# Layer statistics from ScalarE sums, with token routing moved three scan steps, in a two-layer fp32 kernel

## The chip, the cores and the metric

One Trainium2 chip, one of its cores. The metric is the device time of one execution in microseconds (us); lower is better. PE is TensorE, DVE is VectorE, ACT is ScalarE, POOL is GpSimd, and SP is the engine that only issues DMAs.

## The reference, cut to what matters

Eight sequences of 512 tokens with 256 features go through two layers in fp32. Each layer is attention and then a mixture of eight experts, both behind an adaptive layer norm:

```python
h = _layernorm(x) * (1 + ca) + sa
x = x + ga * _L0_attn_ref(h, ...)      # delta rule: a scan over the 512 tokens
h = _layernorm(x) * (1 + cb) + sb
x = x + gb * _L0_ffn_ref(h, ...)       # top-1 expert of 8, 256 -> 1024 -> 256
h = _layernorm(x) * (1 + ca) + sa
x = x + ga * _L1_attn_ref(h, ...)      # causal softmax attention with relative bias
h = _layernorm(x) * (1 + cb) + sb
x = x + gb * _L1_ffn_ref(h, ...)       # all 8 experts, weighted
```

The scan of layer 0 cannot be split over tokens: every step reads the state that the step before it wrote,

```python
retrieved = jnp.einsum('bnhd,bnd->bnh', M, k_t)
delta = v_t - retrieved
M = M + b_t[..., None, None] * jnp.einsum('bnh,bnd->bnhd', k_t, delta)
```

and `_layernorm` subtracts the mean of a token's 256 features and divides by sqrt(variance + 1e-5).

## The kernel before, in words

**Layer 0** goes by chunks of 128 tokens of all eight sequences, i = 0 to 3. `scan` (L731) makes one chunk's 128 steps on DVE. A step is four dependent instructions: a product (L741), a sum over it (L745), an outer product (L751) and the state's update (L756). Everything else of layer 0 is cut into pieces and hung on the steps: `run` (L1366) takes a list of (place, piece), and after step s it traces the pieces whose place is at most s. Within such a piece only the DVE instructions are tied to the step (`tc.issue_after(step)`); they may not come ahead of it. The other engines take theirs from a queue in an order that a list scheduler fixes when the kernel is built: mostly the order of the trace, with a later piece ahead where its inputs and its PSUM bank are free earlier by the scheduler's own estimate. [...] Seven PSUM banks serve all pieces in turn (`bank`).

While chunk i is scanned, three things share its steps:

- `front(i + 1)` normalizes and projects the next chunk's tokens, two sequences at a time: `stats(p)` at place 47 + 8p (sums on ACT, L498 to L509, ending in the square root `sda`), `normal(p)` six places later on DVE (L525), `turn` and `project` behind it. So normal(p) lies at places 53, 61, 69 and 77.
- `follow(i - 1)` does the chunk before: `attend` (places 0 to about 50; `rest` adds the branch to `x1` on POOL at 25 to 28 and 42 to 45, `stats` takes each row block's mean and variance on DVE at 30 to 33 and 46 to 49), then `route`, which is a generator with six parts at places 34, 42, 51, 57, 60 and 62: norm, transposes and gate logits of sequences 0 to 3 and of 4 to 7, the argmax and a prefix count. The last part yields the slots, and `scatter` sends the rows to DRAM by expert. Then `experts` works 15 tiles of 128 rows: `fetch` (L1149, POOL) gathers a tile's two weight blocks of about 1 MB each, `turn` loads and transposes the rows, L1195 and L1204 make the hidden layer, L1216 the output; L1221 copies it to SBUF on ACT, L1222 adds the bias on POOL, L1223 stores it to `ys`. Of the 15 tiles 11 (12 for chunk 2) start in the same scan at place 70 + 4.6 j (4.3 j), the others in the next one.
- The last chunk's `follow(3)` has no scan to hide in and runs in a stretch of its own (the tail of layer 0), together with what is left of chunk 2's experts and with the gathers (L1235) that bring each chunk's `ys` back into token order, multiply by the gate (L1271) and add to `x2` in DRAM (L1272). The gathers of chunks 0 and 1 use eight rows of one tile; those of chunk 2 use `yrow`, a tile with two buffers, with one row in flight (`DEPTH`).

**Layer 1** goes by sequences b: 16 steps of `scores`, `turn` and `weigh`, with `prologue(b + 1)` and `tail(b - 1)` hung between them. `tail` normalizes heads and projects them (`project`, POOL adds L1549, L1550), takes statistics of all four row blocks at place 6.6 (`statistics`, L120 to L134), makes the features (L172 to L183) and gate logits (L1568) from 7.6 on, then the weights at 14 and `experts(i)` (L1621, L1626) from 17 on. Sequence 7's tail comes after the last step; the experts of sequence 6 (places 135, 136.9, 138.8 and 148.8 in its count) lie between its pieces, which start at 134.

Of the kernel before, what the change touches and what calls it, by code (L numbers as in the profile page):

```python
# [20 lines left out]
B = 8  # L21
# [42 lines left out]
def tile_two_layers(ctx: ExitStack, tc: tile.TileContext, t: dict, out: bass.AP):  # L64
# [213 lines left out]
    with ExitStack() as l0:  # L278
# [477 lines left out]
                yield nc.vector.tensor_sub(M, M, upd).ins  # L756


        DEPTH = (3, 3, 1, 1)


        issued = {}
# [1 line left out]
        def attend(i, qk, V, x1, norms):  # L764
# [180 lines left out]
            def stats(b):  # L945
                h = b // 4
                if b % 4 == 0:
                    got["mv", h] = fp.tile([P, 4, 2], F32, tag="mvf", name=f"mvf{i}_{h}")
                st = fp.tile([P, 6], F32, tag="stf", name=f"stf{i}_{b}", bufs=4)
                nc.vector.bn_stats(st, x1[b])  # L950
                nc.vector.bn_aggr(got["mv", h][:, b % 4, :], st)
                if b % 4 == 3:
                    norms.append((got["mv", h], deviation(fp, "f", got["mv", h])))

            pieces = [(0, deltas), (1, tokens)]
            for b in range(B):
# [9 lines left out]
            for h in range(2):  # L966
                pieces.append((16 * h + 25, lambda h=h: roots(h)))
                for b in range(4 * h, 4 * h + 4):
                    pieces.append((13 * h + 25 + b, lambda b=b: rest(b)))
                    pieces.append((12 * h + 30 + b, lambda b=b: stats(b)))  # L970
            return got, pieces

        def route(i, h, norms):
# [29 lines left out]
                room = room.rearrange("p s a b -> p (s a b)")  # L1003
                turned_back = [room[:, b * D : (b + 1) * D] for b in range(B)]
            for half in range(2):
                rs, off = scale_offset(fp, "f", *norms[half])
                pl = bank()
                turned = None
                for n in range(5):
                    b = 4 * half + n  # L1010
                    if n < 4:
                        hb = xn[b]
                        nc.scalar.activation(
                            hb, h[b], AF.Identity, bias=off[:, n : n + 1], scale=rs[:, n : n + 1]
                        )
                        pt = bank()
                        for c in range(2):
                            nc.tensor.transpose(
                                pt[:, c * P : (c + 1) * P], hb[:, c * P : (c + 1) * P], ident
                            )  # L1020
                        hT = fp.tile([P, 2, P], F32, tag="hTf", name=f"hTf{i}_{b}", bufs=2)
                        for c in range(2):
                            by, plus = scale[0][:, 1, c, b : b + 1], shift[0][:, 1, c, b : b + 1]
                            if i == NT - 1 and c == 1:
                                nc.vector.tensor_scalar(
                                    hT[:, c, :], pt[:, c * P : (c + 1) * P], by, plus,
                                    ALU.mult, ALU.add,
                                )
                            else:
                                nc.scalar.activation(  # L1030
                                    hT[:, c, :], pt[:, c * P : (c + 1) * P], AF.Identity,
                                    bias=plus, scale=by,
                                )
                    if n > 0:
                        for k in range(2):
                            nc.tensor.matmul(
                                pl[:, (n - 1) * NE : n * NE], turned[:, k, :], gw[:, k, :],
                                start=(k == 0), stop=(k == 1),
                            )
                        back = bank()  # L1040
# [15 lines left out]
                if half == 0:  # L1056
                    yield
# [81 lines left out]
        def experts(i, slot, idx, scatter):  # L1139
# [46 lines left out]
            for j in range(NSLOT):  # L1186
# [31 lines left out]
                        start=(f == 0), stop=(f == NFC - 1),  # L1218
                    )
                ysb = fp.tile([P, D], F32, tag="ysb", name=f"ysb{i}_{j}", bufs=2)  # L1220
                nc.scalar.copy(ysb, py[:, :D])  # L1221
                nc.gpsimd.tensor_add(ysb, ysb, w[:, NFC * D :])  # L1222
                nc.gpsimd.dma_start(ys_d[i][j * P : (j + 1) * P, :], ysb)  # L1223
                if j != NSLOT - 3:
                    fetch(j + 2, 0)
                if i == NT - 1 and j == NSLOT // 2:
# [32 lines left out]
            queue = []  # L1259
            for b in range(B + DEPTH[i]):  # L1260
                if b < B:
                    if i < NT - 2:
                        yr = w1["fetched"][:, b * D : (b + 1) * D]
                    else:
                        yr = fp.tile([P, D], F32, tag="yrow", name=f"yrow{i}_{b}", bufs=2)
                    with tc.issue_after(issued["fetch"]):
                        gather(b, yr)
                    queue.append(yr)
                if b >= DEPTH[i]:
                    yr, k = queue.pop(0), b - DEPTH[i]  # L1270
                    nc.gpsimd.tensor_mul(yr, yr, gates[1][:, k, :])  # L1271
                    nc.gpsimd.dma_start(x2d[k][i], yr, accum_op=ALU.add)  # L1272
                yield

        def follow(i, qk, V):


            x1, norms = [], []
            _, pieces = attend(i, qk, V, x1, norms)
            work = {}  # L1280

            def begin():
                work["route"] = route(i, x1, norms)
# [12 lines left out]
            def behind():  # L1296
                with tc.issue_after(issued["attention"]):
                    on()

            pieces += [(34, begin), (42, more), (51, more), (57, more), (60, more), (62, settle)]  # L1300

            late, pace, starts = {
                NT - 1: (0, 4, [(10 * j, 10 * j + 3) for j in range(NSLOT)]),
                NT - 2: (12, 4.3, [(43, 62.1), (62.2, 62.4), (62.5, 62.7)]),
            }.get(i, (11, 4.6, [(8, 11), (22, 25), (40, 43), (62.2, 62.7)]))
            pieces += [(62.3, on), (62.6, on)]
            rest = []
# [115 lines left out]
    with ExitStack() as l1:  # L1425
# [76 lines left out]
        def tail(b, got):  # L1502
# [48 lines left out]

                nc.sync.dma_start(y2d[b][i], xs[:, i, :])

            def statistics():
                if b == B - 1:
# [4 lines left out]
                else:  # L1560
                    hT.append(lp.tile([P, 2, S], F32, tag="hTd", name=f"hTd{b}", bufs=1))
                stats.update(enumerate(row_stats("d", [xs[:, i, :] for i in range(NT)])))

            def logits(i):
                cols = slice(i * P, (i + 1) * P)
# [72 lines left out]
            yield from ((7.6 + k, piece) for k, piece in enumerate(made))  # L1638
            yield 14, weights
            yield 15.4, weights_T  # L1640

# [150 lines left out]
```

## Time and profile before

| | |
|---|---|
| median of 3 runs | 2165.22 us (2160.56 to 2169.86) |
| the profiled execution's own time | 2157.99 us |
| its span | 2156.3 us |
| mean granted PE clock | 0.883 |
| PE busy | 1698.6 us (79%) |
| DVE busy | 1577.8 us (73%) |
| ACT busy | 1078.8 us (50%) |
| POOL busy | 641.0 us (30%) |

The profiled execution lies 7.2 us under the median of the runs. Times in the profile count from the start of the span. The scans of chunks 0 to 3 start at 52.0, 298.2, 554.5 and 813.3 us and the last ends at 1067 us; the tail of layer 0 goes on to about 1310 us, and layer 1 fills the rest. In a listing, "out<-in" are tiles by name, brackets hold the engine's idle time before an instruction and what ended it, and a busy digit is tenths of one of 40 slices (53.9 us each).

### The profile page before, as it was taken

To read this page: it belongs to the slowest core of one execution; us is meant where nothing else is said; L and a number is where in the kernel's file an instruction comes from. 1 tells how busy PE (TensorE), PEld (TensorE's weight loads), DVE (VectorE), ACT (ScalarE), POOL (GpSimd) and SP (SyncE) were. 2 spreads that over 40 slices of the span, in tenths; PEclk is the share of its full clock that TensorE was granted. 3 is DMA by queue.
4 is the path that set the end of the run, shared out by engine and by line. 5 is a ranking of instruction groups with operands and counts; after the bars stand their busy time and mean duration, and the time that the engine had idled before them with its cause. 6 is when DMAs were issued, how large, how long until landed. Compare 5 with 4: busy or idle time off the path is not lost. (4 is left out here: it accounts for less than half of the span.)

```text
span 2156.3 us, 32495 instructions
## 1 busy us (share of the span) xinstructions
PE 1698.6 (79%) x10882; PEld 1193.8 (55%) x10882; DVE 1577.8 (73%) x4523; ACT 1078.8 (50%) x2674; POOL 641.0 (30%) x922
## 2 busy tenths in 40 slices
PE   5332137479786997849898798999999999999988
PEld 4211125369674786639777685555555555555543
DVE  4999999989989899899762004677676766776754
ACT  4253125474356744513343236776656574747431
POOL 1223014265354653623365643010111101010220
PEclk8666567699897998959998999999999999999998
DMA  5110000178202681118775873000101010000111
GB/s 169 50 51 5 0 1 11 33 258 303 77 14 81 252 325 50 48 69 321 238 128 196 274 241 74 1 20 9 29 13 25 14 23 13 23 16 11 19 20 14
DMA packets 88679, 189.62 MB, mean 88 GB/s; under 512 B 13712, under 2 KB 67152, under 8 KB 75712
## 3 DMA queue, kind: packets, MB, share of 16 engines
q0 software_dynamic: 33696, 137.43, 19.9%
q1 hardware_dynamic: 54816, 50.11, 8.1%
q8 instruction: 86, 1.41, 0.3%
q14 instruction: 81, 0.66, 0.1%
HBM read 175.12 MB, written 36.93 MB: 98 GB/s over the span
## 5 line engine op out<-in xcount | busy, mean ns | idle before, releaser
L1459 ACT ACTIVATE pr<-sc,low 128x384 f32<-128x384 f32 (+3 forms) x512 | 255.4, 555 | 183.2 <-DVE low L1454 180.8
L1454 DVE CUSTOM_DVE_ANT_0 sc<-ps,strips 128x384 f32<-128x384 f32 (+3 forms) x512 | 225.2, 485 | 95.1 <-PE ps L1445 63.4
L1195 PE MATMUL ps<-hTs,w 128*128 128x128 f32 x1920 | 242.5, 288 | 16.3 <-DMA w<-in_wrows,idx 11.2
L1195 PEld LDWEIGHTS ps<-hTs,w 128*128 128x128 f32 x1920 | 237.6, 203 | 24.2 <-issue 12.2
L745 DVE TENSOR_REDUCE state<-terms 128x16 f32<-128x272 f32 x512 | 227.3, 444 | 15.5
L1216 PE MATMUL ps<-w,act 128*128 128x256 f32 x960 | 226.5, 391 | 15.1 <-DMA w<-in_wrows,idx 12.4
L756 DVE TENSOR_TENSOR state<-state,upd 128x256 f32<-128x256 f32 x511 | 222.4, 435 | 15.0
L1621 PE MATMUL ps<-ew,hTd 128*128 128x512 f32 x512 | 230.5, 605 | 0.0
L741 DVE TENSOR_TENSOR terms<-state,K 128x256 f32<-128x256 f32 x512 | 216.2, 422 | 14.7
L751 DVE TENSOR_TENSOR upd<-K,state 128x256 f32<-128x256 f32 x511 | 214.4, 420 | 16.0
L1216 PEld LDWEIGHTS ps<-w,act 128*128 128x128 f32 x960 | 184.1, 197 | 41.5 <-issue 7.9
L1204 ACT ACTIVATE act<-ps,w 128x128 f32<-128x128 f32 x480 | 136.6, 371 | 139.4 <-PE ps L1195 138.4
L1471 PE MATMUL ps<-cst,pr 128*128 128x128 f32 x1280 | 189.2, 292 | 17.6 <-DVE low L1454 14.5
L1471 PEld LDWEIGHTS ps<-cst,pr 128*128 128x128 f32 x1280 | 146.8, 147 | 86.2 <-DVE low L1454 27.2
L1626 DVE SCALAR_TENSOR_TENSOR accd<-ps,wtd,accd 128x256 f32<-128x256 f32 x256 | 123.5, 482 | 78.0 <-PE ps L1621 70.6
L1630 POOL TENSOR_TENSOR accd<-accd,bc_g 128x256 f32<-128x256 f32 x28 | 20.4, 728 | 527.6 <-DVE accd L1626 527.6
L1621 PEld LDWEIGHTS ps<-ew,hTd 128*128 128x128 f32 x512 | 97.2, 194 | 113.6 <-issue 101.6
L1149 POOL DMA_INDIRECT w<-in_wrows,idx x120 | 123.8, 1032 | 100.0 <-ACT hTs L1173 38.8
L1445 PE MATMUL ps<-kT,qTc 32*128 32x128 f32 (+3 forms) x1024 | 130.6, 486 | 3.8 <-DVE low L1454 2.1
L1480 DVE COPY prT<-ps 128x512 f32<-128x512 f32 (+3 forms) x256 | 117.1, 484 | 8.7 <-PE ps L1471 8.2
L1478 ACT COPY prT<-ps 128x512 f32<-128x512 f32 (+3 forms) x256 | 98.6, 413 | 6.6 <-PE ps L1471 5.8
L1492 PE MATMUL ps<-prT,v 128*32 128x512 f32 (+3 forms) x1024 | 97.5, 452 | 0.0
(297 smaller groups left out, 2855.1 us busy)
## 6 DMA issues: line engine op xcount, KB each, us to landing
hs<-zero SPq DMA_DIRECT2D x4, 1920.0 KB
hslot<-hs SPq DMA_DIRECT2D x60, 128.0 KB
ys<-ysb POOLq DMA_DIRECT2D x60, 128.0 KB, 4.6
x<-in_x SPq DMA_DIRECT2D x32, 128.0 KB
strips<-strip_d SPq DMA_DIRECT2D x16, 256.0 KB
out<-accd POOLq DMA_DIRECT2D x32, 128.0 KB, 3.0
wm<-in_wmod SPq DMA_DIRECT2D x4, 768.0 KB
xt<-in_x SPq DMA_DIRECT2D x12, 256.0 KB
```

The source lines that it names most:

```text
L741: nc.vector.tensor_mul(term[:, :, :HD], M, K[:, s, :].unsqueeze(1).to_broadcast([P, HD, HD]))
L745: nc.vector.tensor_reduce(delta, term, AX.X, ALU.add)
L751: nc.vector.tensor_mul(upd, K[:, s, :].unsqueeze(2).to_broadcast([P, HD, HD]), delta.unsqueeze(1).to_broadcast([P, HD, HD]),)
L756: yield nc.vector.tensor_sub(M, M, upd).ins
L1195: nc.tensor.matmul(ph[:, q * P : (q + 1) * P], w[:, k * FF + f * P : k * FF + (f + 1) * P], hT[:, k, :], start=(k == 0), stop=(k == 1),)
L1204: nc.scalar.activation(act[:, f, :], ph[:, q * P : (q + 1) * P], AF.Relu, bias=w[:, 2 * FF + f : 2 * FF + f + 1],)
L1216: nc.tensor.matmul(py[:, :D], act[:, f, :], w[:, f * D : (f + 1) * D], start=(f == 0), stop=(f == NFC - 1),)
L1445: made = nc.tensor.matmul(pscs[r][:, :W], qT[rows, g, o, i * P : (i + 1) * P], kT[rows, g, :W], start=True, stop=True,)
L1454: nc.vector.tensor_tensor_reduce(out=sc[:, :W], in0=pscs[r][:, :W], in1=strips[:, n, S - W :], scale=1.0, scalar=3.0e38, op0=ALU.add, op1= ...
L1459: nc.scalar.activation(pr, sc[:, :W], AF.Exp, bias=low, scale=-1.0)
L1471: nc.tensor.transpose(pt[:, (i - j) * P : (i - j + 1) * P], prs[r, i][:, j * P : (j + 1) * P], ident,)
L1621: nc.tensor.matmul(pe, hT[0][:, k, cols], ew[:, k, e : e + 2, :], start=(k == 0), stop=(k == 1),)
```

## The change

1. In chunks 0 to 2, `stats` leaves DVE. For each pair of row blocks ACT makes a Copy pass with a running sum, scales the sum to minus the mean, makes a Square pass with that as bias and a running sum, and after four blocks one square root. These pieces lie at 34, 36, 50 and 52.
2. In chunks 0 to 2 the parts of `route` lie at 37, 46, 54, 61, 63 and 65, and what follows moves with them: the first fetches at 65.3 and 65.6, the tiles at 71.5 + 4.6 j (4.3 j), the leftover tiles' pieces that lay between 62.1 and 62.7 at 65.1 to 65.7.
3. The gathers of chunk 2 use eight rows of one tile (`rows`), with two rows in flight.
4. The last tile of chunk 3 adds its bias on DVE straight from PSUM, and SP stores it.
5. In the tail of sequence 7 the statistics come in two halves, at 3.6 and 5.6, and the features start at 4.2.

```diff
-        DEPTH = (3, 3, 1, 1)
+        DEPTH = (3, 3, 2, 1)
...
-                st = fp.tile([P, 6], F32, tag="stf", name=f"stf{i}_{b}", bufs=4)
-                nc.vector.bn_stats(st, x1[b])
-                nc.vector.bn_aggr(got["mv", h][:, b % 4, :], st)
-                if b % 4 == 3:
-                    norms.append((got["mv", h], deviation(fp, "f", got["mv", h])))
+                mv = got["mv", h]
+                if i == NT - 1:
...
+                elif b % 2:
+                    less = bank()
+                    pair = slice(b % 4 - 1, b % 4 + 1)
+                    for k in (b - 1, b):
+                        nc.scalar.activation(
+                            less[:, (k % 2) * D : (k % 2 + 1) * D], x1[k], AF.Copy,
+                            accum_out=mv[:, k % 4, 0:1],
+                        )
+                    nc.scalar.mul(mv[:, pair, 0], mv[:, pair, 0], -1.0 / D)
+                    for k in (b - 1, b):
+                        nc.scalar.activation(
+                            less[:, (k % 2) * D : (k % 2 + 1) * D], x1[k], AF.Square,
+                            bias=mv[:, k % 4, 0:1], accum_out=mv[:, k % 4, 1:2],
+                        )
+                    if b % 4 == 3:
+                        sd = fp.tile([P, 4], F32, tag="sdf", name=f"sdf{i}_{h}")
+                        nc.scalar.activation(
+                            sd, mv[:, :, 1], AF.Sqrt, bias=ln_eps, scale=1.0 / D
+                        )
+                        norms.append((mv, sd))
...
-                    pieces.append((12 * h + 30 + b, lambda b=b: stats(b)))
+                    wait = 3 if i < NT - 1 else 0
+                    pieces.append((12 * h + 30 + b + wait, lambda b=b: stats(b)))
...
-                rs, off = scale_offset(fp, "f", *norms[half])
+                if i == NT - 1:
+                    rs, off = scale_offset(fp, "f", *norms[half])
+                else:
...
+                    nc.vector.reciprocal(rs, sd)
+                    nc.vector.tensor_mul(off, mv[:, :, 0], rs)
...
-                nc.scalar.copy(ysb, py[:, :D])
-                nc.gpsimd.tensor_add(ysb, ysb, w[:, NFC * D :])
-                nc.gpsimd.dma_start(ys_d[i][j * P : (j + 1) * P, :], ysb)
+                rows = ys_d[i][j * P : (j + 1) * P, :]
+                if (i, j) == (NT - 1, NSLOT - 1):
+                    nc.vector.tensor_add(ysb, py[:, :D], w[:, NFC * D :])
+                    nc.sync.dma_start(rows, ysb)
+                else:
...
-                    if i < NT - 2:
-                        yr = w1["fetched"][:, b * D : (b + 1) * D]
-                    else:
-                        yr = fp.tile([P, D], F32, tag="yrow", name=f"yrow{i}_{b}", bufs=2)
+                    room = w1["fetched" if i < NT - 2 else "rows"]
+                    yr = room[:, b * D : (b + 1) * D]
...
-            pieces += [(34, begin), (42, more), (51, more), (57, more), (60, more), (62, settle)]
+            if i == NT - 1:
+                routing = (34, 42, 51, 57, 60)
+            else:
+                routing = (37, 46, 54, 61, 63)
+            pieces += zip(routing, (begin, more, more, more, more))
+            pieces.append((62 if i == NT - 1 else 65, settle))
...
-                NT - 2: (12, 4.3, [(43, 62.1), (62.2, 62.4), (62.5, 62.7)]),
-            }.get(i, (11, 4.6, [(8, 11), (22, 25), (40, 43), (62.2, 62.7)]))
-            pieces += [(62.3, on), (62.6, on)]
+                NT - 2: (12, 4.3, [(43, 65.1), (65.2, 65.4), (65.5, 65.7)]),
+            }.get(i, (11, 4.6, [(8, 11), (22, 25), (40, 43), (65.2, 65.7)]))
+            pieces += [(65.3, on), (65.6, on)]
...
-                        pieces.append((70 + pace * (j + half / 2), on))
+                        pieces.append((71.5 + pace * (j + half / 2), on))
...
-            yield 6.6, statistics
+            if b == B - 1:
+                yield 3.6, lambda: statistics((0, 1))
+                yield 5.6, lambda: statistics((2, 3))
+                begin = 4.2
+            else:
+                yield 6.6, lambda: statistics(tuple(range(NT)))
+                begin = 7.6
```

More of the change, by code (lines that the diff above doesn't have):

```diff
@@ L948, in stats @@
                     got["mv", h] = fp.tile([P, 4, 2], F32, tag="mvf", name=f"mvf{i}_{h}")
[L949 to L953 removed]
+                mv = got["mv", h]
+                if i == NT - 1:
+                    st = fp.tile([P, 6], F32, tag="stf", name=f"stf{i}_{b}", bufs=4)
+                    nc.vector.bn_stats(st, x1[b])
+                    nc.vector.bn_aggr(mv[:, b % 4, :], st)
+                    if b % 4 == 3:
+                        norms.append((mv, deviation(fp, "f", mv)))
+                elif b % 2:
[12 more added lines that the diff above has]
+                        )
+                    if b % 4 == 3:
+                        sd = fp.tile([P, 4], F32, tag="sdf", name=f"sdf{i}_{h}")
[3 more added lines that the diff above has]
+                        norms.append((mv, sd))
             pieces = [(0, deltas), (1, tokens)]
@@ L1005, in route @@
             for half in range(2):
-                rs, off = scale_offset(fp, "f", *norms[half])
+                if i == NT - 1:
+                    rs, off = scale_offset(fp, "f", *norms[half])
+                else:
+                    mv, sd = norms[half]
+                    rs, off = (
+                        fp.tile([P, 4], F32, tag=f"{tag}f", name=f"{tag}f{i}_{half}")
+                        for tag in ("rs", "off")
+                    )
+                    nc.vector.reciprocal(rs, sd)
+                    nc.vector.tensor_mul(off, mv[:, :, 0], rs)
                 pl = bank()
@@ L1220, in experts @@
                 ysb = fp.tile([P, D], F32, tag="ysb", name=f"ysb{i}_{j}", bufs=2)
-                nc.scalar.copy(ysb, py[:, :D])
-                nc.gpsimd.tensor_add(ysb, ysb, w[:, NFC * D :])
-                nc.gpsimd.dma_start(ys_d[i][j * P : (j + 1) * P, :], ysb)
+                rows = ys_d[i][j * P : (j + 1) * P, :]
[3 more added lines that the diff above has]
+                else:
+                    nc.scalar.copy(ysb, py[:, :D])
+                    nc.gpsimd.tensor_add(ysb, ysb, w[:, NFC * D :])
+                    nc.gpsimd.dma_start(rows, ysb)
                 if j != NSLOT - 3:
@@ L1552, in project, with statistics @@
                 nc.sync.dma_start(y2d[b][i], xs[:, i, :])
-            def statistics():
-                if b == B - 1:
+            def statistics(tiles):
+                if not hT and b == B - 1:
                     hT.append(
@@ L1559, in statistics @@
                     )
-                else:
+                elif not hT:
                     hT.append(lp.tile([P, 2, S], F32, tag="hTd", name=f"hTd{b}", bufs=1))
-                stats.update(enumerate(row_stats("d", [xs[:, i, :] for i in range(NT)])))
+                tag = "d" if len(tiles) == NT else "c"
+                stats.update(zip(tiles, row_stats(tag, [xs[:, i, :] for i in tiles])))
             def logits(i):
@@ L1637, in tail @@
             )
-            yield from ((7.6 + k, piece) for k, piece in enumerate(made))
+            yield from ((begin + k, piece) for k, piece in enumerate(made))
             yield 14, weights
```

## The prediction

> **What bounds the kernel now.** I read the page first. The scan lasts from 52 to 1067 us, and there DVE is near full in every slice:
>
> ```profile
> DVE  4999999989989899899762004677676766776754
> ACT  4253125474356744513343236776656574747431
> ```
>
> The second row says that ACT, which is to take over work, is about half busy there. Being near full is not yet a price, so next the DVE timeline of a scan step with a statistics pair and, after "...", of the end of a bare one (columns: start, length, engine, line, operation):
>
> ```profile
> 916.52 0.43 DVE L756 TENSOR_TENSOR state<-state,upd 128x256 f32<-128x256 f32 x1
> 916.86 0.41 DVE L950 BATCH_NORM_STATS2 stf<-x 128x6 f32<-128x256 f32 x1
> 917.20 0.41 DVE L741 TENSOR_TENSOR terms<-state,K 128x256 f32<-128x256 f32 x1
> 917.52 0.17 DVE L951 BATCH_NORM_AGGREGATE mvf<-stf 128x2 f32<-128x6 f32 x1
> ...
> 918.57 0.43 DVE L756 TENSOR_TENSOR state<-state,upd 128x256 f32<-128x256 f32 x1
> ...
> 920.62 0.43 DVE L756 TENSOR_TENSOR state<-state,upd 128x256 f32<-128x256 f32 x1
> 921.09 0.42 DVE L741 TENSOR_TENSOR terms<-state,K 128x256 f32<-128x256 f32 x1
> ```
>
> L756 to L756 is 2.05 us with a pair (916.52, 918.57, 920.62); bare steps are 1.86 us apart. So a pair whose instructions last 0.41 and 0.17 us lengthens a step by 0.19 us. L756 to L741 is 0.47 us bare and 0.68 us with L950 between: the chain waits for its own results, and an independent instruction mostly fills that wait.
>
> Third, the waits of DVE during the scans of chunks 1 to 3 (total, times, longest):
>
> ```profile
> DVE rsa L525 <- ACT sda L509: 9.7, 5, 4.9
> DVE dm L930 <- POOL bdM L931: 4.8, 4, 1.4
> DVE ms L934 <- ACT ms L919: 4.0, 3, 2.0
> ```
>
> The longest are two waits of normal(3) for `sda`: 4.86 us at 461.2 (chunk 1) and 3.65 us at 720.5 (chunk 2). ACT's timeline ahead of the first:
>
> ```profile
> 450.09 1.14 ACT L1204 ACTIVATE act<-ps,w 128x128 f32<-128x128 f32 x4 [3.87 <-PE ps L1195]
> 452.36 1.14 ACT L1204 ACTIVATE act<-ps,w 128x128 f32<-128x128 f32 x4 [1.13 <-PE ps L1195]
> ...
> 453.58 0.40 ACT L498 ACTIVATE ps<-xt 128x256 f32<-128x256 f32 x1
> ...
> 460.87 0.29 ACT L509 ACTIVATE sda<-mva,cst 128x2 f32<-128x2 f32 x1
> ```
>
> stats(3), at place 71, stands behind the first tile's activations, at place 70, which wait for PE.
>
> From 1067 us on PE takes over: it is busy 58.4 of 64 us (1066 to 1130), then 119.2 of 136 us (1170 to 1306). In that last stretch POOL and PE wait for:
>
> ```profile
> POOL yrow L1235 <- DMA x<-yrow: 10.9, 4, 5.4
> POOL yrow L1271 <- DMA yrow<-ys,slot: 4.5, 3, 3.2
> ```
> ```profile
> PE ps L1195 <- DMA w<-in_wrows,idx: 7.7, 6, 4.5
> PE ps L1216 <- DMA w<-in_wrows,idx: 7.2, 3, 3.5
> ```
>
> POOL issues the weight fetches, so its stalls make them late. Layer 1 is PE's (713.9 of 737 us); the change touches only its end, where PE idles 6.03 us for sequence 7's statistics:
>
> ```profile
> 2103.51 0.69 PE L179 MATMUL ps<-cst,xnd 128*128 128x128 f32 x2 [6.03 <-ACT xnd L172]
> ```
>
> **What the Trainium skill says.** "VectorE: DVE Perf Modes", section The DRAIN you can't avoid, says that the next operation does not start until the pipe is empty, and to minimize the count of operations. By that, 24 pairs at 0.59 us would give 14 us; the intervals above give a third, and I take the trace. "ScalarE: Activation LUTs", section Table sets, says that cheap functions are in every set, so Copy and Square need no load; the trace agrees (L498 and L504 have none of their own; a load of L509 lasts 1.283 us). "DMA: Bandwidth & Descriptors", section Anatomy of one DMA, gives about 2.0 us fixed; the last `ys` store takes 1307.07 to 1309.09, 2.02 us.
>
> **The change part by part.**
>
> *Statistics off DVE.* 8 pairs in each of three chunks, at 0.19 us: 1.5 us a chunk. Reciprocal and product stay (0.17 and 0.15 us). In chunks 1 and 2 (the scans in which chunks 0 and 1 are routed) it is on the path: -3.1. In chunk 3 PE sets the end: nothing there.
>
> *The same on ACT.* A row block costs what L498 and L504 with their accumulator reads show, spaced 0.31 + 0.22 + 0.41 + 0.22 = 1.16 us: 4.8 us a half with the small ones. It lands where ACT was idle: 7.8 us at 356 to 364, 13.6 us waiting for the last L951 (387 to 401), 6.1 us in the next scan. Behind it in the queue are attention's copies; cover gone, a half would cost up to 4.8 us. I take 0.
>
> *Routing three steps later, chunks 1 and 2.* The first tile moves from 70 to 71.5, behind stats(3) at 71, and its data come 3 x 1.86 = 5.6 us later. stats(3) needs only its bank and `xt`, so ACT should take it first: of 4.86 + 3.65 = 8.5 us I take -7.0 (0 to -8.5). In exchange, half 1 of the gate (8 us of ACT work, 404.7 to 413.8) slides from 51 to 54, onto stats(1), whose `sda` was already 0.3 to 0.4 us late at place 61. And argmax to prefix count shrinks from three steps to two, leaving PE some 1.2 us for a matmul pair that now takes 0.8 us behind other work. No row shows either; up to 5.6 us a scan for the first, below nothing since attention's last pieces now precede the gate (the `ms` waits of these two scans, 2.0 and 1.0 us, could go). The scheduler put rows late where it expected inputs late, so I take +2.0 (-3 to +11).
>
> POOL's eight scatters and first fetches (10 us) and SP's row loads move along; tiles then run to about place 121 of 128, so only the start of the next scan gets PE work, where PE idles.
>
> *Routing later, chunk 3.* PE is full from the first tile (969.4) to the scan's end and into the tail, so a late start is paid in full. The slots were ready at 946.9, but POOL stood before tile 14's output (L1222 at 950.05) and began to scatter at 951.92. Slots 5.6 - 1.5 = 4.1 us later come at 951.0: nothing lost, unless tile 14 slips too; then up to 5.6. I take +2.0.
>
> *Rows and depth.* POOL's 15.4 us of gather stalls go. The PE waits directly behind them are 3.5 (fetch issued 1203.0 after a stall of 5.4) and 4.5 us (fetch issued 1229.4 after one of 4.0); others follow transfers that took 7 to 8 us without a stall. If DMA bandwidth is the limit, nothing is won: 0 to -9, I take -4.5.
>
> *Last bias.* After the last L1216 (1305.5) come ACT's copy, POOL's add (1306.05, 0.72 us) and POOL's issue at 1307.07. One DVE add (0.42 us, as L1548, also from PSUM) and SP's issue (0.32) would start the store at about 1306.15: -0.9. DVE and SP have nothing else then (DVE is busy 3.3 of the last 136 us), and the gather behind it is on the path: PE idles 4.88 us until 1315.55 for its rows. If the SP store landed later than POOL's, this could be 0.
>
> *Halves.* Block 1's `xs` is done at 2091.4, so blocks 0 and 1 get their norm while sequence 6's experts hold PE (2089.6 to 2096.5). After the last `xs` at 2101.4 only blocks 2 and 3 are left. PE's first transpose stays at 2103.5; the copies of four blocks, 1.67 us apart, now end at 2110.1, 6.6 us later; those of two, back to back from 2104.2 at 0.8 us each, would end at 2105.9: -4.2 (-2 to -5). Behind that come the gate logits, then experts, all shifted as one. Next late is block 3 itself. One more root and reciprocal (0.3 and 0.2 us) lie in ACT's and DVE's idle time.
>
> Sum: -3.1 - 7.0 + 2.0 + 2.0 - 4.5 - 0.9 - 4.2 = **-15.7 us**, so 2158.0 becomes 2142.3; on the median, 7.2 us higher, 2165.2 becomes **2149.5**.
>
> **Rivals.**
>
> *The moves cancel* (stats(3) freed, stats(1) late by as much). For: ACT is busy almost without a break from 413 to 428. Against: DVE's order is the scheduler's. Without the terms -7.0 and +2.0 of the scans: -10.7, 2154.5.
>
> *Nothing reaches the end but halves and bias*: DMA-bound fetches, tile 14 slipping, waits as they were: -3.1 + 5.6 - 0.9 - 4.2 = -2.6, 2162.6. That the change does not do what it says has this look too: the scheduler keeps ACT's old order.
>
> *Slower: ACT's queue keeps routing work ahead of the next chunk's statistics.* Then both `sda`, places 61 and 77, come three steps later in two scans: 4 x 5.6 = 22.3. With -3.1 + 2.0 - 4.5 - 0.9 - 4.2 it is +11.6, 2176.8. It decides once L1204 of the first tile still precedes L498 of stats(3) and DVE reaches L525 first. For it: that order exists now. Against: place 71.5 is behind 71.
>
> **How the numbers follow.** Chances: the sum 0.48, cancelling 0.22, ends only 0.18, slower 0.12. A measurement tells about 0.5% (10.8 us) from no change. The sum's own range, 2140 to 2157, is nine parts in ten faster; cancelling sits on the edge, half and half; ends only is the same; the slower rival mostly slower. Faster 0.54, same 0.35, slower 0.11. The range 2139 to 2167 takes in the first three cases.
>
> **What would show it.** Right: bare steps at 30 to 33; no L525 wait above 1 us near place 77, L498 of stats(3) ahead of the first L1204; PE's `w` waits in the tail's tiles under 11 us; PE's idle before the last features gone and the gap from last `xs` to last logits shorter by 4 us. Wrong: L525 waits at 61, first tile of chunk 3 over 3 us later from its scan's start, or gather stalls gone with PE's waits unchanged.

## The result, and the profile after

The changed kernel takes 2176.67 us, median of 20 runs (2163.94 to 2182.61), against 2161.47 us for the kernel before in the same comparison (20 runs, 2153.86 to 2173.23). The ratio is 1.0064, 95% interval 1.0050 to 1.0079: slower by 0.64%, some 14 us, where 16 us less were predicted. The profiled execution has a span of 2173.0 us (2156.3 before) at a granted PE clock of 0.882 (0.883).

The page's rows of 40 slices for DVE and ACT in the changed kernel (a slice is now 54.3 us):

```profile
DVE  5999999889997999889853004677676766676754
ACT  4253125565467754633343246777566664747431
```

DVE still looks full over the scans, and ACT did not become fuller in any slice by more than a step or two. Seen from here nothing has happened. It is the waits that changed. DVE's waits during the scans of chunks 1 to 3 of the changed kernel (total, times, longest):

```profile
DVE rsa L525 <- ACT sda L509: 10.6, 4, 4.2
DVE over L1124 <- PE ps L1116: 7.3, 2, 4.2
DVE ms L934 <- ACT ms L919: 7.2, 4, 3.9
DVE lg L1084 <- PE ps L1069: 5.6, 2, 2.8
DVE dm L930 <- POOL bdM L931: 5.4, 5, 1.5
```

Together 36.1 us, against 18.5 before. The `rsa` waits are about as long in sum as before (9.7 us), but they lie elsewhere: 3.80 and 4.17 us at step 63 (0.31 and 0.37 us before, at step 62), and only 1.26 and 1.41 us at step 78 (4.86 and 3.65 before). `over` and `lg` did not wait at all before. Counted from the first L741 of each scan (300.4, 556.7 and 815.5 us before, 2.2 us later than the starts given further up), the waits of chunk 1 are 12.0 us (7.2 before), of chunk 2 16.5 (7.5) and of chunk 3 7.6 (3.8), and the scans last 261.5 (256.3), 265.8 (258.8) and 251.1 us (250.1). The last scan ends at 1078.3 us, 12.7 us later than before; from there to the end the changed kernel loses another 4.0 us.

Where do the two new waits of a scan come from? First ACT ahead of step 63 of chunk 1 (start, length, engine, line, and in brackets the idle time and what ended it):

```profile
421.19 0.37 ACT L1081 COPY x<-ps 128x256 f32<-128x256 f32 x1 [2.68 <-PE ps L1075]
421.45 0.40 ACT L498 ACTIVATE ps<-xt 128x256 f32<-128x256 f32 x1
...
428.53 0.30 ACT L509 ACTIVATE sda<-mva,cst 128x2 f32<-128x2 f32 x1
```

L1081 at 421.19 is the last copy of the gate's half 1, which the change moved from place 51 to 54. Only behind it does ACT begin `stats(1)` of the next chunk (L498). DVE needed `sda` from 425.1 us on and had it at 428.8. Then PE, in the same kernel, and the two DVE instructions that waited:

```profile
433.12 3.67 PE L543 MATMUL ps<-wqkv,hT 128*128 128x512 f32 x4 [0.55 <-ACT hT L145]
436.58 1.14 PE L547 MATMUL ps<-wqkv,hT 128*128 128x272 f32 x4
437.56 0.33 PE L1111 MATMUL ps<-pick,cst 128*128 128x64 f32 x2
437.81 0.43 PE L1112 MATMUL ps<-cst,count 64*128 64x64 f32 x2
438.09 0.34 PE L1116 MATMUL ps<-cst,count 64*128 64x8 f32 x2
```
```profile
428.86 0.17 DVE L525 RECIPROCAL rsa<-sda 128x2 f32<-128x2 f32 x1 [3.80 <-ACT sda L509]
...
438.46 0.22 DVE L1124 TENSOR_TENSOR over<-ps,cst 128x64 f32<-128x64 f32 x1 [3.04 <-PE ps L1116]
```

The count's matmuls (L1111 to L1116, 0.9 us in all) had their input at 431.4 us, when DVE's copy L1109 ended. They stand in PE's queue behind a projection of the next chunk (L543, L547, 4.4 us), which comes from the late `rsa` and began at 433.1. Before, the count's matmuls (there L1078 to L1083) stood ahead of this projection:

```profile
422.69 0.33 PE L1078 MATMUL ps<-pick,cst 128*128 128x64 f32 x2
...
427.37 3.50 PE L543 MATMUL ps<-wqkv,hT 128*128 128x512 f32 x4 [0.55 <-ACT hT L145]
430.71 1.08 PE L547 MATMUL ps<-wqkv,hT 128*128 128x272 f32 x4
```
```profile
423.11 0.17 DVE L525 RECIPROCAL rsa<-sda 128x2 f32<-128x2 f32 x1 [0.31 <-ACT sda L509]
```

Does the first wait make the second? Hardly. From the start of L525 to the end of that projection it is 8.9 us in the changed kernel and 8.7 us before, where `rsa` had waited only 0.31 us. DVE comes to L1124 6.6 us after L525. So an `rsa` that is only just in time would still leave a wait of about 2.8 us there (8.7 + 0.7 to the end of the count's matmuls - 6.6; an estimate from these lines). The second wait comes from the order of PE's queue. The Trainium skill, "Perfetto Trace Analysis", section Tensor Engine Instruction, says that ACT and DVE take their queues strictly in order and that PE can pull weight loads ahead of matmuls; these lines agree: L1111 began 6.2 us after its input was there, and PE stood idle for 1.3 us of them.

In the tail of layer 0, PE's waits in the last tiles (1187 to 1325 us) and the ACT instruction behind the largest of them:

```profile
PE ps L1249 <- ACT act L1237: 9.1, 2, 8.8
PE ps L1228 <- DMA w<-in_wrows,idx: 6.1, 5, 2.6
PE ps L1249 <- DMA w<-in_wrows,idx: 1.8, 2, 1.4
```
```profile
1248.24 0.30 ACT L126 ACTIVATE sdc<-mvc,cst 128x3 f32<-128x3 f32 x1 [12.54 <-DVE mvc L121]
```

The waits for weights fell from 14.9 to 7.9 us, as deeper gathers were to make them. But all of PE's waits there are 17.5 us, as before (17.6): ACT stood 12.5 us (2.2 before) for the statistics of layer 1's first tokens, with the activations of a tile behind that in its queue. The loads of these tokens (`xs_first`) were issued at 1232.9 to 1235.0 us and the last was used at 1247.6; before, at 1219.0 to 1221.2 and at 1226.2.

At the end of the kernel come the halves. PE's transposes of block 2, which stand for the line with 6.03 us before:

```profile
2123.75 0.69 PE L179 MATMUL ps<-cst,xnd 128*128 128x128 f32 x2 [3.78 <-ACT xnd L172]
```

From the last `xs` (2121.6) to the end it is 51.4 us, against 55.0 before.

### The profile page after: what moved, and what is told of

Read it like the earlier page. It is cut to its first block, busy times and chain, and to the rows that moved or that the text cites. A ratio compares the mean times of both kernels' runs of the same rounds, so it can differ in the third digit from the quotient of the medians.

```text
span 2173.0 us, 32564 instructions
## 1 busy us (share of the span) xinstructions
PE 1714.9 (79%) x10882; PEld 1201.5 (55%) x10882; DVE 1573.3 (72%) x4478; ACT 1104.8 (51%) x2782; POOL 639.3 (29%) x920
## 3 DMA queue, kind: packets, MB, share of 16 engines
q8 instruction: 86, 1.41, 0.3%
## 5 line engine op out<-in xcount | busy, mean ns | idle before, releaser
L1249 PE MATMUL ps<-w,act 128*128 128x256 f32 x960 | 227.5, 392 | 16.6 <-ACT act L1237 9.8
L756 DVE TENSOR_TENSOR state<-state,upd 128x256 f32<-128x256 f32 x511 | 222.4, 435 | 15.0
L741 DVE TENSOR_TENSOR terms<-state,K 128x256 f32<-128x256 f32 x512 | 216.6, 423 | 15.9
L1249 PEld LDWEIGHTS ps<-w,act 128*128 128x128 f32 x960 | 184.8, 198 | 42.9 <-ACT act L1237 11.8
L1514 PE MATMUL ps<-cst,pr 128*128 128x128 f32 x1280 | 191.0, 293 | 17.6 <-DVE low L1497 14.3
```

What stands on the lines that cost most here:

```text
L741: nc.vector.tensor_mul(term[:, :, :HD], M, K[:, s, :].unsqueeze(1).to_broadcast([P, HD, HD]))
L1249: nc.tensor.matmul(py[:, :D], act[:, f, :], w[:, f * D : (f + 1) * D], start=(f == 0), stop=(f == NFC - 1),)
L1514: nc.tensor.transpose(pt[:, (i - j) * P : (i - j + 1) * P], prs[r, i][:, j * P : (j + 1) * P], ident,)
```

## The experiments

Every ratio is to the kernel before, run on the same chip in the same comparison, with its 95% interval. The kernel before had medians of 2169.23, 2161.14, 2170.31 and 2160.55 us in the four comparisons below.

### First comparison: the parts one by one

The changed kernel with ScalarE's statistics, but all moves undone:

```diff
-                routing = (37, 46, 54, 61, 63)
+                routing = (34, 42, 51, 57, 60)
...
-                    wait = 3 if i < NT - 1 else 0
+                    wait = 0
...
-                        pieces.append((71.5 + pace * (j + half / 2), on))
+                        pieces.append((70 + pace * (j + half / 2), on))
```

> The changed kernel with the routing, the first fetches and the tiles back at their old places (34 to 62, tiles at 70), and the statistics of chunks 0 to 2 still on ScalarE but at 30 to 33 and 46 to 49; rows, bias and halves kept. Theory A (the loss comes from where the routing was moved): the waits of DVE for rsa at step 63, for the count (L1124) at 66 and for the gate's logits (L1084) at 47 are gone or under 1 us, the late sda at step 77 is back (about 4 us in chunks 1 and 2), and the scan ends 10 to 16 us earlier than in the changed kernel: ratio to the kernel before 0.996 to 1.000. Theory B (the loss comes from ScalarE's passes, which hold up what stands behind them in its queue): the scan ends within 4 us of the changed kernel's, ratio 1.004 to 1.008.

Measured: 2174.9 us, ratio 1.0031 (1.0017 to 1.0044). Between the two theories, and so a partial miss for both. The wait for `over` is gone, that for `rsa` near 63 is down to 0.8 and 2.2 us, and the late `sda` near step 77 is back, about as A has it, but other waits came, and the last scan ends at 1086.7 us, 11.8 us later than in the run with the ends alone (the third of this comparison), where A had it 10 to 16 us earlier than in the changed kernel. DVE's waits in chunk 3's scan of this kernel (three of four lines):

```profile
DVE ms L934 <- ACT ms L919: 3.8, 1, 3.8
DVE rsf L1038 <- ACT sdf L973: 3.2, 1, 3.2
DVE lg L1084 <- PE ps L1069: 2.8, 1, 2.8
```

In the run with the ends alone the same scan has only 1.0 us for `ms` and 2.0 for `dm`. So ScalarE's statistics do cost at the old places: the passes lie between attention's last copies and the gate, and DVE now needs their result (`rsf`). The `lg` wait of 2.8 us comes with them, not with the move: the next run has the move and not the passes, and no `lg` wait.

The changed kernel with its moves, but the statistics on DVE:

```diff
-                if i == NT - 1:
+                if True:
                     st = fp.tile([P, 6], F32, tag="stf", name=f"stf{i}_{b}", bufs=4)
...
-                    wait = 3 if i < NT - 1 else 0
+                    wait = 0
```

> The changed kernel with the statistics of chunks 0 to 2 back on DVE at 30 to 33 and 46 to 49, the routing still at 37 to 65 and the tiles at 71.5; rows, bias and halves kept. Theory A: the waits at 63 and 66 stay (together 6 to 8 us in each of chunks 1 and 2), the scan ends where the changed kernel's does or up to 4.6 us later (24 pairs at 0.19 us): ratio 1.006 to 1.009. Theory B: the scan's waits go and the ratio is 0.994 to 1.001.

Measured: 2181.93 us, ratio 1.0061 (1.0044 to 1.0077), as A has it. DVE's waits in chunk 1's scan with the move and DVE's statistics, and then in the run without either:

```profile
DVE rsa L525 <- ACT sda L509: 5.4, 2, 4.0
DVE ms L934 <- ACT ms L919: 3.9, 1, 3.9
DVE over L1124 <- PE ps L1116: 3.0, 1, 3.0
```
```profile
DVE rsa L525 <- ACT sda L509: 5.8, 2, 5.0
DVE ms L934 <- ACT ms L919: 2.7, 1, 2.7
```

The waits at 63 and 66 are the move's own; no pass of ScalarE's statistics is in this kernel.

The kernel before with nothing but the three ends (rows and depth, last bias, halves):

```diff
-        DEPTH = (3, 3, 1, 1)
+        DEPTH = (3, 3, 2, 1)
...
+            if b == B - 1:
+                yield 3.6, lambda: statistics((0, 1))
+                yield 5.6, lambda: statistics((2, 3))
+                begin = 4.2
```

> The kernel before with nothing but rows and depth, the last bias and the halves. By the prediction's terms -4.5 - 0.9 - 4.2 = -9.6 us: ratio 0.9956. The rival from the two traces: the stretch from the scan's end to the first rows of layer 1 did not become shorter (244.2 us before, 246.7 after), so rows and bias give nothing here, and the halves at most 2 to 4 us: ratio 0.998 to 1.000. If the rows alone lengthen that stretch, it shows here as over 245 us.

Measured: 2165.24 us, ratio 0.9983 (0.9968 to 0.9997), 4 us, as the rival has it. In its profile it is 50.7 us from the last `xs` to the end (55.0 before): the halves are as much as the whole gain, and nothing is left that could be put down to rows and bias.

The kernel before with nothing but the tiles' places:

```diff
-                        pieces.append((70 + pace * (j + half / 2), on))
+                        pieces.append((71.5 + pace * (j + half / 2), on))
```

> The kernel before with nothing but the tiles' places at 71.5 + 4.6 j (4.3 j) in place of 70. Theory A (the first tile's activations ahead of stats(3) in ScalarE's queue made the late sda at step 77): the two waits of 4.9 and 3.7 us fall under 1.5 us each, the scan ends 5 to 8 us earlier and the kernel is 2 to 8 us faster: ratio 0.996 to 0.999. Rival: the order on ScalarE is the scheduler's, and stats(3) came ahead only since the routing itself was later: waits as before, ratio 1.000 to 1.002.

Measured: 2166.32 us, ratio 0.9967 (0.9951 to 0.9982), 7 us by the ratio (the medians are only 2.9 us apart). DVE's waits in its chunk 1:

```profile
DVE ms L934 <- ACT ms L919: 2.7, 1, 2.7
DVE rsa L525 <- ACT sda L509: 0.6, 1, 0.6
```

The late `sda` at step 77 is gone with this one number, without any move of the routing. Theory A holds here.

Of these runs: against the ends alone (0.9983), ScalarE's statistics by themselves cost 0.48%, the moves by themselves 0.78%, and both together 0.81% (1.0064, from the comparison above). By this the two don't add; with the changed kernel's ratio of the fourth comparison (1.0094) both together cost 1.1%, so this stays open.

### Second comparison: order against the next chunk's front

The changed kernel with the next chunk's front moved along, so that nothing changes places between the two:

```diff
-                parts, more, _ = front(i + 1, 47 if i > 0 else 30)
+                parts, more, _ = front(i + 1, 50 if i > 0 else 30)
...
-                        pieces.append((71.5 + pace * (j + half / 2), on))
+                        pieces.append(((71.5 if i == NT - 2 else 74.5) + pace * (j + half / 2), on))
```

> The changed kernel with the next chunk's front moved along by the same three steps (its stats(p) at 50 + 8p, normal(p) at 56 + 8p), and the tiles of chunks 0 and 1 at 74.5 (of chunk 2 still at 71.5), so that routing and front keep the order that they had among themselves in the kernel before. Theory A (what costs is where the routing now stands against the front: half 1 of the gate ahead of stats(1) on ScalarE, and the count's matmuls behind the projection of normal(1) on PE): the waits of 3.8 and 4.2 us for rsa and of 3.0 and 4.2 us for over fall under 1 us each, the scan ends 10 to 15 us earlier than in the changed kernel: ratio to the kernel before 0.998 to 1.001. Theory B (ScalarE's passes or the later slots cost): ratio 1.004 to 1.008.

Measured: 2167.14 us, ratio 1.0032 (1.0017 to 1.0048). Half of the loss is back, less than A expected; the ratio lies between the theories. The waits for `rsa` and `over` went as A has it, but others stayed or came, over both scans (four lines of five):

```profile
DVE ms L934 <- ACT ms L919: 6.3, 3, 4.4
DVE count L1109 <- PE ps L1104: 3.7, 2, 2.2
DVE lg L1084 <- PE ps L1069: 3.2, 1, 3.2
...
DVE rsa L525 <- ACT sda L509: 0.2, 1, 0.2
```

The last scan ended at 1064.3 us, 14 us earlier than in the changed kernel. The time fell by less: chunk 2's first tile came 157.0 us after its scan's start (153.9 in the kernel before), and from there to the last gathers PE needed 347.7 us (342.0 in the changed kernel, 331.8 to 346.0 in all the other profiles). Why PE took longer in that execution is not settled.

The same with the statistics on DVE (the edits of the second run above):

> The run with the front moved along, but with the statistics of chunks 0 to 2 on DVE at 30 to 33 and 46 to 49. Set against that run it shows what ScalarE's statistics are worth by themselves once the order is kept. By the prediction's term (16 pairs at 0.19 us on the path) it is 3.1 us slower than that run: ratio higher by 0.0014. If ScalarE's passes cost what they seemed to at the old places (waits for the gate's logits and for ms), it is 3 to 10 us faster than that run.

Measured: 2164.46 us, ratio 1.0015 (0.9999 to 1.0030). ScalarE's statistics against DVE's, order kept: 0.17% slower, with intervals that overlap. Neither sign is shown; a gain of more than a few microseconds is not compatible with them.

The changed kernel with half 1 of the gate, the argmax, the count and the slots earlier:

```diff
-                routing = (37, 46, 54, 61, 63)
+                routing = (37, 46, 52.5, 59, 60.9)
...
-            pieces.append((62 if i == NT - 1 else 65, settle))
+            pieces.append((62 if i == NT - 1 else 64, settle))
```

> The changed kernel with half 1 of the gate at 52.5 in place of 54, the argmax at 59 (61), the count at 60.9 (63), ahead of normal(1) at 61, and the slots at 64 (65). Theory A: the count's matmuls stand ahead of the projection of normal(1), so the waits for over (3.0 and 4.2 us) go, and the wait for rsa at 61 shrinks by about 1.5 steps of 1.86 us to 1 to 2 us; up to 1 us comes for the gate's logits at 59: 8 to 11 us less in all, ratio 1.001 to 1.003. If these waits follow from the length of ScalarE's queue and not from the order, they stay and the ratio is 1.005 to 1.007.

Measured: 2167.2 us, ratio 1.0030 (1.0015 to 1.0044): half of the loss. `over` waits no more, and no wait for `rsa` is seen at step 63 (at 78 it is 2.5 and 2.1 us). But the count itself now waits, 4.2 us in either scan, since its own first matmul (L1104) stands behind a projection in PE's queue. PE, then DVE and ACT in chunk 1:

```profile
426.84 1.08 PE L547 MATMUL ps<-wqkv,hT 128*128 128x272 f32 x4
427.85 0.43 PE L1104 MATMUL ps<-cst,pick 128*64 128x128 f32 x2
```
```profile
428.32 0.28 DVE L1109 COPY count<-ps 64x128 f32<-64x128 f32 x1 [4.20 <-PE ps L1104]
428.53 0.15 DVE L525 RECIPROCAL rsa<-sda 128x2 f32<-128x2 f32 x1
```
```profile
427.84 0.29 ACT L509 ACTIVATE sda<-mva,cst 128x2 f32<-128x2 f32 x1
```

The `sda` still came only at 428.1 us; DVE stood for the count until 428.3, so the late `sda` is covered by this wait and not gone.

The version that follows from the first comparison, the kernel before with the two edits that gained there, the tiles at 71.5 and the three ends, and nothing else:

> The kernel before with the tiles at 71.5, rows and depth, the last bias and the halves, and nothing else of the change: statistics on DVE, routing at 34 to 62. If the gains of the two runs add (0.33% for the tiles' places and 0.17% for the ends): ratio 0.995, 0.993 to 0.997. If the earlier end of the scans is lost again where PE sets the end of layer 0: 0.997 to 0.999.

Measured: 2149.51 us (6 runs), ratio 0.9931 (0.9906 to 0.9957). It beats both kernels: 11.6 us under the kernel before by the medians, 15 us by the ratio. The two gains add, as expected.

### Third comparison: where the deeper gathers' gain went

Rows and depth alone; the same with the loads of `xs_first` two tiles later; these later loads alone; and the best version with them. The second edit is one line:

```diff
-                if i == NT - 1 and j == NSLOT // 2:
+                if i == NT - 1 and j == 9:
```

> The kernel before with nothing but the rows and the depth of chunk 2's gathers. By the prediction's term -4.5 us: ratio 0.998. Theory C (the gathers' stalls on POOL go and PE waits less for weights, but the loads of layer 1's first tokens, `xs_first`, now compete with weight fetches and arrive 10 to 15 us after their issue in place of 5; ScalarE stands at their statistics' square root, L126, with the activations of a tile behind it, and PE waits for these): PE's waits for w in the last tiles fall from 15 to about 8 us and one wait of 6 to 9 us for act takes their place: ratio 0.999 to 1.001.

> The same with the loads of `xs_first` two tiles later (at tile 9 in place of 7, when the gathers of chunk 2 are done). Theory C: the loads take about 5 us again, ScalarE's wait at L126 falls from about 10 us to 2 to 5, PE's wait for act from about 8 to under 3: 4 to 7 us faster than with rows and depth alone, ratio 0.996 to 0.998. Rival (the fetches are bound by the DMA engines, so that PE's waits only move back to w): no faster than with rows and depth alone.

> The kernel before with nothing but the later loads of `xs_first`: the control of the run above. Before, ScalarE waited only 2.2 us at L126 and PE 1.0 us for act behind it, so there is little to win: ratio 0.9990 to 1.0005. If it is as fast as the run with rows and the later loads, the rows are worth nothing even so.

> The run with the tiles at 71.5 and the three ends (0.9931 of the kernel before), with the loads of `xs_first` at tile 9. In that run's profile ScalarE waited 10.2 us at L126 and PE 8.8 us for act in the last tiles. Theory C: these go, 4 to 8 us, ratio 0.989 to 0.992. Rival: ratio as without, 0.993.

Measured, in this order: 0.9992 (0.9971 to 1.0012), 0.9994 (0.9979 to 1.0009), 1.0011 (0.9991 to 1.0030) and 0.9938 (0.9919 to 0.9958). Rows and depth alone bring nothing that can be told (the interval takes in the predicted 4.5 us as well as none), and their profile shows the exchange that theory C names (PE in the last tiles, two of the lines):

```profile
PE ps L1216 <- ACT act L1204: 8.0, 3, 6.5
PE ps L1195 <- DMA w<-in_wrows,idx: 5.0, 5, 2.5
```

The remedy failed. With later loads ACT still stood 6.3 to 6.5 us at L126 in each of the three runs, and no time was won. That the exchange happens is shown; that ACT's wait is what keeps the gain from the end is not. The rival, that the waits only change their name, fits as well.

### Fourth comparison: chunk 2's branch

The changed kernel with chunk 2's branch (in chunk 3's scan, where no front runs) as in the kernel before; the changed kernel itself; and the run with front along and DVE's statistics, with chunk 2's routing and tiles as before. The first edit, in all places alike:

```diff
-            if i == NT - 1:
+            if i >= NT - 2:
                 routing = (34, 42, 51, 57, 60)
```

> The changed kernel, but with chunk 2's branch (statistics, routing and tiles, in chunk 3's scan) as in the kernel before: DVE statistics, parts of the routing at 34 to 62, tiles from 70. Chunks 0 and 1 as changed. If the later slots cost in chunk 3 what the traces show (first tile 157.0 us after its scan's start in four kernels with the move, 153.2 in four without): 3 to 5 us faster than the changed kernel, 0.15 to 0.25%. By the prediction's term: 2 us. If the tail takes it up: no difference.

> The changed kernel itself, on the chip of the other two: ratio 1.005 to 1.008 as measured. In its profile the waits for rsa at step 63, for over at 66 and for the gate's logits at 47 come again with the same lengths within 0.5 us, if they come from the order of the queues.

> The run with the front moved along and DVE's statistics (ratio 1.0015), with chunk 2's routing and tiles as in the kernel before. What is left of the change is then the move in chunks 0 and 1, with its order against the front kept, and the ends. If the rest of the loss was chunk 3's late slots: 4 to 8 us faster than that run, ratio 0.998 to 1.000. If it lies in chunks 1 and 2 (attention's last root, 3.9 us at step 42): 1.001 to 1.002 as it was.

Measured: 2165.72 us, 1.0020 (1.0002 to 1.0038); 2179.31 us, 1.0094 (1.0068 to 1.0119, 6 runs); 2157.31 us, 0.9982 (0.9964 to 1.0001). The changed kernel's own ratio is a little higher than at first; the intervals overlap. Its new waits came again to 0.1 us: 3.79 and 4.18 us at step 63, 3.04 and 4.19 at 66, 2.78 at 47. They belong to the kernel, not to one execution. The first run of this comparison has the same order in chunks 1 and 2, and there `rsa` waits 3.29 and 4.96 us and `over` 3.80 and 3.04: a longer first wait does not bring a longer second one.

Chunk 2's branch put back gives 13.6 us in one pair of medians and 7.2 us in the other (1.0015 to 0.9982, over two comparisons): more than the 3 to 5 us of the expectation in both, and well above the prediction's 2. The first pair also puts chunk 2's statistics back on DVE; in the second only routing and tiles differ.

## Why the prediction was wrong

**The new waits, +2.0 (-3 to +11): the term that failed.** They are 17.2 us in the two scans: 7.3 more for `rsa` at 63, 7.3 for `over`, 2.6 more for `ms`, which it thought could go (another 2.8 for `lg` belong to the passes, below). The prediction saw both main candidates and their places, half 1 of the gate on `stats(1)` and the count's shorter time on PE. It priced the first at up to 5.6 us a scan (3.5 and 3.8 came) and the second only as 0.8 us of matmuls in a gap of 1.2 us. It did not ask which work of PE would stand in front of them once the front's projection was due; the answer is 4.4 us of it, which ends 8.9 us after `rsa` where DVE needs the count after 6.6. Then it took a middle value near zero, on the argument that the scheduler would order by estimated arrivals. The order was fixed at build time, and as run it made DVE wait.

**Routing later in chunk 3, +2.0 (0 to 5.6): too small.** "Nothing lost, unless tile 14 slips too": it did. Tile 14 began 122.3 us into that scan before and 130.6 after, and the scatter no longer waits for its output but for the slots, which came at 138.0 in place of 131.2 us. The first tile came 155.9 us after its scan's start, 153.9 in the profile of before; on one chip it was 156.0 with the change and 150.9 with chunk 2's branch put back, 5.1 us. In time the branch cost 7 to 14 us, the 7 in the pair in which only routing and tiles differ; that is more than its first tile shows, and the rest is not resolved. Nor is the move alone in making the slots late: in the run with ScalarE's statistics at the old places they came at 137.0 us and the first tile at 157.5, against 130.5 and 151.7 with the ends alone.

**The same statistics on ACT, 0: wrong.** The idle stretches named as cover could not be used. The 7.8 us at 356 to 364 are still there, since ACT waits in it for PE at the head of its queue and the passes stand behind that; they ran from 368.0 us on, between attention's copies. In chunks 2 and 3 they made the gate's start late: its reciprocal (`rsf`) ran at step 43 in every kernel with the move and these passes there, and at 37 in those with the move and DVE's statistics. The logits come 10 us after it and are due at step 47, hence the `lg` wait of 2.8 us.

**Statistics off DVE, -3.1: not seen in the time.** Bare steps did come at these places (1.85 us from L756 to L756 at 363.86 and 365.71), and the three scans grew by 4.4 us less than their waits, about what 24 pairs at 0.19 us give. But between the two runs with the front along the same difference is 0.8 us the other way, and by the ratios the whole exchange cost 0.03% with the moves (over two comparisons; 0.33% with the changed kernel's later ratio), 0.17% with front along and 0.48% at the old places. No gain. The section of the Trainium skill against which the prediction sets the 0.19 us ("VectorE: DVE Perf Modes", The DRAIN you can't avoid) itself adds that a next operation which is not held starts earlier, so page and trace are less far apart than the prediction says. And where the prediction says that Copy and Square need no load, the page that it cites there lists copy among the cheap functions and not Square; for Square the trace alone speaks.

**The freed `sda`, -7.0 (0 to -8.5): right.** The two waits fell by 5.8 us in the changed kernel (1.26 and 1.41 us are left, just over the 1 us set as the sign), and the one number 71.5 alone gives 7 us by the ratio, 3 by the medians.

**Rows and depth, -4.5 (0 to -9): the first half of the mechanism was right, the gain is none to be told** (0.9992 alone, 0.9971 to 1.0012). PE's `w` waits fell by 7.0 us, and a wait for `act` of the same size took their place, which the prediction did not have. **Last bias, -0.9: right:** from the last tile's start to the first gather 11.5 us before, 10.2 after. **Halves, -4.2 (-2 to -5): right:** 3.6 us in the changed kernel, 4.3 in the run with the ends alone.

**The slower rival**, given a chance of 0.12, had 2176.8 us, and 2176.67 was measured. The agreement is chance: of its two late `sda` only the first came, the one at 77 was freed, and waits behind PE's queue and ACT's passes, which it did not have, stand in their place; the kernel before was also some 4 us faster than the 2165.2 from which it counts. Of the signs set in advance, the `rsa` wait at 61 and the gather stalls gone with PE's waits unchanged both said wrong. Of the signs of being right the bare steps, `w` waits under 11 us and most of the shorter end came.

The kernel with the tiles' places and the ends alone also had 2149.51 us, the very number predicted. That too is chance in part: its kernel before had 2161.1 us and not 2165.2, and its terms in the prediction add up to -16.6 us, of which the -4.5 for rows and depth were not confirmed. What it shows is that the terms that were right made a faster kernel without those for which the change had been made.

## What to carry to other kernels

When a piece of work is moved in time, its own length is the smaller part of the price: list for each in-order queue what it will then stand in front of and behind, and count the longest of these through to its end (here 8.9 us from a reciprocal to the end of the projection that it feeds, against 6.6 us until DVE needed what stood behind it). Idle time of an engine is no cover where the head of its queue is what waits, as in the 7.8 us here. Split a change of several parts early; here the tiles' places and the ends made the best kernel, and the parts that the change was made for took it back.

## What was not expected of the hardware

In the comparisons in which the kernel before took 2169 to 2170 us, and in none of those in which it took 2161, each profile shows ACT standing once for 5.3 to 7.4 us in chunk 2's scan for something that the trace calls only "remote", with PE's work done by the profile. It came with kernels of old and new order, mostly at the second half of chunk 0's last tile, once at another instruction. What it waits for is not known. It is as long as most effects studied here, so single profiles from different chips should not be subtracted without looking for it. Nor is the rest steady: from the last gathers to the end, where the kernels differ by little but the halves, the profiles lie between 841.4 and 854.1 us.
